# Blocks of edges two at a time on VectorE, one three-sum combine of x, and one addition for an odd tile's k and v

## The chip, the core and the metric

One core of one Trainium2 chip runs the whole kernel. The engines are named as in the profile: PE is TensorE's matmul, PEld its weight load, DVE is VectorE, ACT is ScalarE, POOL is GpSimd (it issues the indirect DMAs, the gathers and scatters by row number), SP is SyncE (it issues plain DMAs). The metric is the device time of one execution in microseconds; the median of several runs counts.

## The reference

Graph attention with a residual and a layer norm, for 16 batches of 1024 nodes with 512 features and 8 heads of 64. The adjacency is one matrix of zeros and ones for all batches. It is sparse and skewed: node i's chance of an edge falls with its number.

```python
q, k, v = (x @ W + b).reshape(b, n, H, HD)  for W, b of q, k and v
scores = einsum('bqhd,bkhd->bhqk', q, k) / sqrt(HD)
scores = scores + (1.0 - adj)[None, None, :, :] * -1000000000.0
attn = softmax(scores, axis=-1)
out = einsum('bhqk,bkhd->bqhd', attn, v).reshape(b, n, d)
x = layernorm(x + out @ Wo + bo, axis=-1)
```

## The kernel before

The kernel does not build the 1024 x 1024 scores. It sorts the nodes by their number of edges, at the start and on the chip, and then works on **blocks**: one block is 128 edges, one for each of 128 query nodes, so a block needs 128 rows of q on the 128 partitions and the 128 rows of k and v at the other ends of the edges, which POOL gathers from DRAM. There are 530 blocks over the 16 batches, in a list `blocks`. A block's steps, with the tiles they write:

- `gather(n)`: POOL fetches a `kvg` tile of 128 rows, k in columns 0 to 511 and v in the rest. It is issued eight turns ahead (`AHEAD`). The tag `kvg` has 8 buffers.
- `products(n)`: DVE multiplies q (`qt`, or `qg` where it was gathered as well) with k into `qk`, line 1313.
- `scores(n)`: DVE sums that by head, 128 x 512 to 128 x 8, into `s`, line 1317.
- `exponentials(n)`: ACT, into the last 8 columns of a `pv` tile, line 1328.
- `weigh(n)`: v times these, by ACT in 8 instructions (line 1341) or by DVE in one (line 1345).
- `add_own(n)` on DVE (line 1357) or `add_up(n)` as two matmuls on PE (`sum`, lines 1366 and 1367) put a tile's blocks together; `normalise` divides, a transpose makes `oT`, and four matmuls with `wo` (`po`, line 799) and the layer norm finish the tile.

**PE's other half** is q, k and v for all rows. q is four matmuls a tile (`pq`, also line 799). For k and v, two tiles of 128 rows (`pair(b, j)`, tiles 2j and 2j + 1 of batch b, four pairs a batch) go together in a scheme of seven half products in place of eight: combinations of the weights (`t1` to `t4`) and of x (`s1` to `s4`, each 128 x 256, made in `combine` by four DVE instructions, lines 783 to 786) are made beforehand, and afterwards DVE adds the results up. Each half product is two matmuls of 128 x 512, four records in the trace. They go in this order, with what follows each on another engine one turn later:

- x (`b11`), then ACT copies it to `e` (line 969)
- p6 (`t2`), then DVE makes `w` = p6 + e (line 972)
- the four matmuls of q of the even tile
- x (`b21`) on top of the first, then ACT copies the even tile's k out of it (line 835)
- p7 (`t3`), then DVE makes `g` = p7 + w (line 975)
- transposes of the next pair's x (`pxT`)
- z (`t1`), then the odd tile's v = z + g (line 984)
- the four matmuls of q of the odd tile (none in the first pair of a batch after the first)
- p4 (`t4`), then the odd tile's k = p4 + g (line 979)
- z (`b22`) on top of the first z, once line 984 has read it, then the even tile's v = z + w (line 988)

x and z are one PSUM tile each, with one buffer; p6, p7, p4 and everything else share four `fill` banks; `sum` has two.

**What sets the order.** The program is written out by a loop over turns n. In each turn the steps above are issued for blocks near n in a fixed order (exponentials of n + 3, products of n + 4, gathers, weighing of n + 1, adding of n, scores of n + 4, then whatever earlier steps planned for this turn with `later`), and then PE gets matmul units from two lists, `finishing` (`po`) and `fronts` (the pairs), as many as its share of the turn allows. A unit is issued only when its `ready` condition holds. The engines then run their lists strictly in order, and semaphores set by the tile framework hold them where a tile isn't written or free.

Of the kernel before, what the change touches and what calls it, by code (L numbers as in the profile page):

```python
# [31 lines left out]
KG_BUFS, Q_BUFS, QT_BUFS, PV_BUFS, Y_BUFS = 8, 5, 3, 5, 6  # L32
# [146 lines left out]
def kernel(  # L179
# [75 lines left out]
    with ExitStack() as main:  # L255
# [101 lines left out]
        def loads():  # L357
# [26 lines left out]
            nc.vector.tensor_tensor(T2, B22, T1, op=OP.subtract)  # L384
            combined.append(True)
            yield
            nc.vector.tensor_tensor(T3, B22, B12[0], op=OP.subtract)
# [73 lines left out]
        def ranks():  # L461
            yield
            for t in range(NT):
                ADJ.append(work.tile([P, N], F32, tag="kvg", name=f"adj_{t}", bufs=KG_BUFS))
                nc.gpsimd.dma_start(ADJ[t], adj[ds(t * P, P), :])
# [171 lines left out]
        def edges(t):  # L637
            nb, J, K = BLOCKS[t], DEGREE[t], OWN[t]
            tag, bufs = ("kvg", KG_BUFS) if J > 16 else ("kv", 5)
            v = work.tile([P, N], F32, tag=tag, name=f"codes_{t}", bufs=bufs)  # L640
# [60 lines left out]
            for i0 in range(0, nb, step):  # L701
# [8 lines left out]
                m = work.tile([P, D], F32, tag="qk", name=f"em_{t}_{i0}", bufs=2)[:, 0:n * J].rearrange("p (n j) -> p n j", n=n)  # L710
# [27 lines left out]
        X, XT, SX, KV, VSUM, NRM, Y, OT, PS = {}, {}, {}, {}, {}, {}, {}, {}, {}  # L738
# [13 lines left out]
        def transpose_x(b, t):  # L752
            def pe():
# [5 lines left out]
                def out():  # L759
                    XT[b, t] = work.tile([P, D], F32, tag="xT", name=f"xT_{b}_{t}", bufs=4)  # L760
# [19 lines left out]
                def combine():  # L780
                    s = [work.tile([P, HD2], F32, tag=f"s{i}", name=f"s{i}_{b}_{t}", bufs=1 + i // 4) for i in (1, 2, 3, 4)]
                    x0, x1 = XT[b, t - 1], XT[b, t]
                    nc.vector.tensor_tensor(s[0], x1[:, 0:HD2], x1[:, HD2:D], op=OP.add)
                    nc.vector.tensor_tensor(s[2], x0[:, 0:HD2], x1[:, 0:HD2], op=OP.subtract)
                    nc.vector.tensor_tensor(s[1], s[0], x0[:, 0:HD2], op=OP.subtract)
                    nc.vector.tensor_tensor(s[3], x0[:, HD2:D], s[1], op=OP.subtract)
                    SX[b, t // 2] = s
# [23 lines left out]
        def norm(b, t, k):  # L811
            if b not in NRM:
                NRM[b] = work.tile([P, NT, NPAIR], F32, tag="nrm", name=f"nrm_{b}", bufs=2)
            squares(f"k_{b}_{t}", k, NRM[b][:, t, :])

        def pair(b, j):
# [131 lines left out]
            def unit(bank, left, right, first, after, need):  # L948
                def pe():
                    if first:  # L950
                        R[bank] = fill_psum(f"p{bank}_{b}_{j}") if bank[0] == "p" else psum.tile(
                            [P, HALF], F32, tag=bank, name=f"{bank}_{b}_{j}", bufs=1
                        )
# [8 lines left out]
                return [(2 * PRODUCT, pe, lambda: (need is None or need in R) and (b, j) in SX and bool(combined))]  # L962
# [13 lines left out]

            def out_k1():
                kv = KV[b, tt[1]]
                nc.vector.tensor_tensor(kv[:, 0:D], R["p4"], R["g"], op=OP.add)  # L979
                send(1)  # L980
                later_last(1, lambda: norm(b, tt[1], kv[:, 0:D]))
# [5 lines left out]
            def out_v0():  # L987
                nc.vector.tensor_tensor(KV[b, tt[0]][:, D:], R["z"], R["w"], op=OP.add)
                send(0)
# [5 lines left out]
            units += unit("x", lambda: a(0, 0), B11, True, out_e, None)  # L995
            units += unit("p6", s(2), T2, True, out_w, None)
            units += q0
            units += unit("x", lambda: a(0, 1), B21, False, lambda: out_k(0, R["x"]), "e")
            units += unit("p7", s(3), T3, True, out_g, None)
            units += xt  # L1000
            units += unit("z", s(1), T1, True, out_v1, None)
            units += q1
            units += unit("p4", lambda: a(1, 1), T4, True, out_k1, None)
            units += unit("z", s(4), B22, False, out_v0, "v1")
            return units

        loaded, half, wide = {}, [], []
# [196 lines left out]
        KG, QG, PV, PSUM, QT, RDEN, V1 = {}, {}, {}, {}, {}, {}, {}  # L1204
# [45 lines left out]
        def gather(n):  # L1250
# [33 lines left out]
            else:  # L1284
                g = first[t] + i - OWN[t]
                tag, bufs = ("qt", Q_BUFS) if fronts or i % 2 else ("xT", 4)
                QG[n] = work.tile([P, D], F32, tag=tag, name=f"qg_{n}", bufs=bufs)
                gather_q(QG[n], b, (query_row if b else query_row0)[:, g:g + 1])
            tag, bufs = ("kvg", KG_BUFS) if fronts or n % 5 % 2 == 0 else ("kv", 5)
            KG[n] = work.tile([P, 2 * D], F32, tag=tag, name=f"kvg_{n}", bufs=bufs)  # L1290
# [9 lines left out]
        QK = {}  # L1300

        def products(n):
            b, t, i = blocks[n]
            if t == 0 and i == 0 and b < PAIRED_FROM:
                norms = small.tile([P, NPAIR], F32, tag="lone", name=f"lone_{b}", bufs=1)
                later_last(0, lambda q=QT[b, t]: squares(f"q_{b}", q, norms, lone))
                later(2, lambda: nc.vector.tensor_reduce(lone_norm[:, b:b + 1], norms, axis=AX.X, op=OP.max))
            if i < OWN[t]:
                q = QT[b, t] if i < OWN[t] - 1 else QT.pop((b, t))
            else:  # L1310
                q = QG.pop(n)
            QK[n] = work.tile([P, D], F32, tag="qk", name=f"qk_{n}", bufs=2)
            nc.vector.tensor_tensor(QK[n], q, KG[n][:, 0:D], op=OP.mult)  # L1313
# [344 lines left out]
```

## Time and profile before

| what | value |
|---|---|
| three timed runs | 1853.99, 1860.07, 1872.71 us, median 1860.07 |
| span of the profiled execution | 1840.4 us (its own time outside the span is not given) |
| busy PE, DVE, ACT, POOL | 1798.2, 1693.7, 1563.2, 1215.3 us |
| granted PE clock, mean | 0.996 |
| DMA | 303 GB/s, mean |

The span runs from the first to the last instruction of the profiled execution; the timed runs also hold what lies around it. Busy times are unions of the instructions' spans, and neighbouring instructions of one engine overlap at their ends, so the start-to-start distance, not the duration, tells what an instruction costs in a row.

### The profile page before, as it was taken

What the parts mean: (1) busy time and instruction counts of PE and PEld (TensorE: products, weight loads), DVE (VectorE), ACT (ScalarE), POOL (GpSimd) and SP (SyncE); (2) the same over time, 40 slices, a digit from 0 to 9 for tenths busy, and PEclk for the clock granted to TensorE, in tenths of its full rate; (3) what the DMA queues carried; (4) which work ended last, traced back from release to release, by engine and by line L of the source; (5) the groups of instructions that cost most, each with busy time, mean ns of one, the idle gap of its engine ahead of it and who ended that gap; (6) DMA issues with size and microseconds to landing.
All of it is one profiled execution on the core that took longest, in us unless ns stands there. A gap on an engine that the chain in (4) does not pass through costs nothing.

```text
span 1840.4 us, 25352 instructions
## 1 busy us (share of the span) xinstructions
PE 1798.2 (98%) x5140; PEld 876.2 (48%) x5140; DVE 1693.7 (92%) x3473; ACT 1563.2 (85%) x6183; POOL 1215.3 (66%) x1142
## 2 busy tenths in 40 slices
PE   7999999999999999999999999999999999999997
PEld 3444454554444454444444445444544444444443
DVE  6889889999989999999999999999999999997986
ACT  3637869989889898999889988989799999987886
POOL 1367766766565776767757666677666767665786
PEclk9999999999999999999999999999999999999998
DMA  7358787989889899999988998999989999889995
GB/s 287 106 190 253 256 325 237 346 301 327 308 280 314 295 336 319 344 316 308 347 316 310 346 335 276 343 321 322 339 315 325 314 355 326 306 324 325 338 319 191
DMA packets 198791, 558.54 MB, mean 303 GB/s; under 512 B 33450, under 2 KB 33470, under 8 KB 198626
## 3 DMA queue, kind: packets, MB, share of 16 engines
q0 software_dynamic: 112640, 370.50, 59.3%
q1 hardware_dynamic: 82910, 180.52, 26.2%
q10 hardware_dynamic: 3076, 5.82, 0.9%
q14 instruction: 122, 1.00, 0.2%
q8 instruction: 43, 0.70, 0.2%
HBM read 420.30 MB, written 157.45 MB: 314 GB/s over the span
## 4 chain that ended last, share of the span: by engine, by line
PE 69%; DVE 10%; ACT 9%; DMA 4%; issue 3%; POOL 1%; SPq 0%; POOLq 0%; DVEq 0%; ACTq 0%
PE po L799 17%; PE pq L799 15%; PE pp L956 12%; PE z L956 9%; PE x L956 9%; ACT pv L1341 5%; DVE qk L1313 2%; PE poT L1401 2%; PE pxT L757 2%; PE sum L1367 2%; DVE s L1317 2%; PE sum L1366 2%; DVE pv L1357 1%; ACT sq_k L809 1%; DMA kvg<-kv_pair,place_row 1%
## 5 line engine op out<-in xcount | busy, mean ns | idle before, releaser
L1341 ACT ACTIVATE pv<-kvg,pv 128x64 f32<-128x64 f32 x3600 | 907.5, 341 | 0.0
L1292 POOL DMA_INDIRECT kvg<-kv_pair,place_row x462 | 526.7, 1140 | 307.4 <-ACT pv L1341 99.6
L799 PE MATMUL pq<-wq,xT 128*128 128x512 f32 x792 | 367.8, 596 | 0.0
L1317 DVE TENSOR_REDUCE s<-qk 128x8 f32<-128x512 f32 x530 | 360.7, 681 | 6.8
L799 PE MATMUL po<-wo,oT 128*128 128x512 f32 x792 | 359.3, 594 | 0.7 <-ACT oT L1405 0.7
L1313 DVE TENSOR_TENSOR qk<-qt,kvg 128x512 f32<-128x512 f32 x434 | 297.2, 685 | 1.1 <-DMA kvg<-kv_rows,key_row 0.6
L956 PE MATMUL x<-b,xT 128*128 128x512 f32 x504 | 237.3, 593 | 0.5 <-ACT e L969 0.4
L956 PE MATMUL pp<-t,s 128*128 128x512 f32 x504 | 237.0, 593 | 0.0
L1357 DVE TENSOR_TENSOR pv<-pv,pv 128x520 f32<-128x520 f32 x329 | 228.3, 694 | 4.3 <-ACT pv L1341 4.2
L799 PEld LDWEIGHTS po<-wo,oT 128*128 128x128 f32 x792 | 149.1, 191 | 170.0 <-issue 160.2
L799 PEld LDWEIGHTS pq<-wq,xT 128*128 128x128 f32 x792 | 148.4, 192 | 161.9 <-issue 149.9
L1010 POOL DMA_INDIRECT x<-in_x_dram,asked_row x120 | 133.0, 1108 | 77.8 <-issue 21.3
L1148 POOL DMA_INDIRECT out_dram<-y,asked_row x129 | 146.9, 1139 | 39.1 <-issue 21.2
L1328 ACT ACTIVATE pv<-s,absent 128x8 f32<-128x8 f32 x434 | 127.0, 294 | 44.0 <-DVE s L1317 40.8
L809 ACT ACTIVATE sq_k<-kv 128x128 bf16<-128x128 f32 x512 | 150.8, 301 | 6.4 <-DVE kv L979 3.4
L956 PEld LDWEIGHTS pp<-t,s 128*128 128x128 f32 x504 | 94.7, 191 | 108.1 <-issue 99.4
L956 PEld LDWEIGHTS x<-b,xT 128*128 128x128 f32 x504 | 94.2, 191 | 107.4 <-issue 99.0
L956 PE MATMUL z<-b,s 128*128 128x512 f32 x252 | 119.2, 596 | 7.0 <-DVE kv L984 7.0
L1246 POOL DMA_INDIRECT qg<-q_rows,query_row x96 | 104.4, 1088 | 28.4 <-issue 26.9
L956 PE MATMUL z<-t,s 128*128 128x512 f32 x252 | 118.6, 593 | 0.0
L956 PE MATMUL pp<-t,xT 128*128 128x512 f32 x252 | 118.5, 593 | 0.0
L1134 ACT ACTIVATE y<-y,stats 128x512 f32<-128x512 f32 (+1 forms) x128 | 102.7, 806 | 17.0 <-DVE stats L1129 17.0
(279 smaller groups left out, 2713.0 us busy)
## 6 DMA issues: line engine op xcount, KB each, us to landing
kv_pair<-kv SPq DMA_DIRECT2D x98, 512.0 KB
q_rows<-q SPq DMA_DIRECT2D x106, 256.0 KB
qt<-q_rows SPq DMA_DIRECT2D x98, 256.0 KB
residual<-x SPq DMA_DIRECT2D x83, 256.0 KB
y<-residual SPq DMA_DIRECT2D x83, 256.0 KB
kv_rows<-kv SPq DMA_DIRECT2D x15, 512.0 KB
kvg<-kv_pair,place_row POOLq DMA_INDIRECT x462, 6.9
kv_pair<-kv SPq DMA_DIRECT2D x28, 256.0 KB
```

What stands on the lines that cost most here:

```text
L799: nc.tensor.matmul(p, lhs(c), w[:, c, :], start=(c == 0), stop=(c == NPAIR - 1))
L809: nc.scalar.activation(sq, s[:, ts(h, P)], AF.Square, scale=scale, accum_out=sums[:, h:h + 1])
L956: nc.tensor.matmul(R[bank], l[:, ts(c, P)], right[:, c, :], start=(first and c == 0), stop=(c == 1), skip_group_check=True,)
L1010: nc.gpsimd.indirect_dma_start(out=y, out_offset=None, in_=x_rows, in_offset=bass.IndirectOffsetOnAxis(ap=asked_row[:, t:t + 1], axis=0), ...
L1148: nc.gpsimd.indirect_dma_start(out=out_rows[b, t], out_offset=bass.IndirectOffsetOnAxis(ap=rows, axis=0), in_=y, in_offset=None, element_o ...
L1246: nc.gpsimd.indirect_dma_start(out=q, out_offset=None, in_=q_rows[b % ROWS], in_offset=bass.IndirectOffsetOnAxis(ap=rows, axis=0))
L1292: nc.gpsimd.indirect_dma_start(out=KG[n], out_offset=None, in_=rows, in_offset=bass.IndirectOffsetOnAxis(ap=(place_row if b else key_row)[ ...
L1313: nc.vector.tensor_tensor(QK[n], q, KG[n][:, 0:D], op=OP.mult)
L1317: nc.vector.tensor_reduce(S[n], QK.pop(n).rearrange("p (h d) -> p h d", d=HD), axis=AX.X, op=OP.add)
L1328: nc.scalar.activation(PV[n][:, D:], S.pop(n), AF.Exp, bias=bias)
L1341: nc.scalar.activation(pv[:, ts(h, HD)], v[:, ds(D + h * HD, HD)], AF.Copy, scale=pv[:, D + h:D + h + 1])
L1357: nc.vector.tensor_tensor(PV[b, t], PV[b, t], pv, op=OP.add)
```

## The change

Three things change, and with them the tiles that carry them.

**Blocks two at a time.** `kvg` tiles become pairs, 4 of twice the size. `products` is called at odd turns for the blocks n + 3 and n + 4. Where both have the same q, one DVE instruction multiplies 128 x 2 x 512; otherwise two do. The product is written over k in `kvg`, and `qk` goes. `scores` sums both blocks in one instruction (128 x 16). Exponentials come at n + 2, after which the weighing by ACT follows in the same turn; gathers move behind DVE's weighing.

**Three sums of x.** The signs are turned so that s1 and s3 have one operand in common and can be made by one instruction of 2 x 256 into a tile `s31`. The transposed x of both tiles, too, lies in one tile of two halves.

**One addition for k and v.** x and z become the two halves of one PSUM tile `xz`, made once for the whole kernel. In the last three pairs of a batch p4 goes into the x half instead of a fill bank, moves ahead of z (`t1`), and one DVE instruction adds g to both halves, 1024 columns, into the odd tile's k and v. The first pair keeps two additions. A list `freed` tells `ready` that the step that reads a half has been issued.

The diff, cut to the parts that the prediction speaks of:

```diff
+        XZ = psum.tile([P, 2, HALF], F32, tag="xz", name="xz", bufs=1)
+        freed = []
...
-                    s = [work.tile([P, HD2], F32, tag=f"s{i}", name=f"s{i}_{b}_{t}", bufs=1 + i // 4) for i in (1, 2, 3, 4)]
-                    x0, x1 = XT[b, t - 1], XT[b, t]
-                    nc.vector.tensor_tensor(s[0], x1[:, 0:HD2], x1[:, HD2:D], op=OP.add)
-                    nc.vector.tensor_tensor(s[2], x0[:, 0:HD2], x1[:, 0:HD2], op=OP.subtract)
-                    nc.vector.tensor_tensor(s[1], s[0], x0[:, 0:HD2], op=OP.subtract)
-                    nc.vector.tensor_tensor(s[3], x0[:, HD2:D], s[1], op=OP.subtract)
+                    nc.vector.tensor_tensor(
+                        s31, both[:, :, 0:HD2], both[:, 1, :].rearrange("p (a d) -> p a d", a=2), op=OP.subtract
+                    )
+                    nc.vector.tensor_tensor(s2, both[:, 0, 0:HD2], s31[:, 1, :], op=OP.subtract)
+                    nc.vector.tensor_tensor(s4, both[:, 0, HD2:], s2, op=OP.subtract)
...
-                    if first:
-                        R[bank] = fill_psum(f"p{bank}_{b}_{j}") if bank[0] == "p" else psum.tile(
-                            [P, HALF], F32, tag=bank, name=f"{bank}_{b}_{j}", bufs=1
-                        )
+                    if first and bank in at:
+                        R[bank] = XZ[:, at[bank], :]
+                    elif first:
+                        R[bank] = fill_psum(f"p{bank}_{b}_{j}")
...
-                return [(2 * PRODUCT, pe, lambda: (need is None or need in R) and (b, j) in SX and bool(combined))]
+                return [(2 * PRODUCT, pe, lambda: all(k in R or k in freed for k in need) and (b, j) in SX and bool(combined))]
+
+            at = {"x": 0, "z": 1, "p4": 0} if j else {"x": 0, "z": 1}
...
+            def out_kv1():
+                kv = new_kv(1)
+                nc.vector.tensor_tensor(
+                    kv.rearrange("p (w d) -> p w d", w=2), XZ, R["g"][:, None, :].to_broadcast([P, 2, D]), op=OP.add
+                )
...
             def out_v0():
                 nc.vector.tensor_tensor(KV[b, tt[0]][:, D:], R["z"], R["w"], op=OP.add)
+                freed.append(("v", b, j))
                 send(0)
...
-            units += xt
-            units += unit("z", s(1), T1, True, out_v1, None)
-            units += q1
-            units += unit("p4", lambda: a(1, 1), T4, True, out_k1, None)
-            units += unit("z", s(4), B22, False, out_v0, "v1")
+            if j:
+                units += q1[:1] + xt
+                units += unit("p4", lambda: a(1, 1), T4, True, lambda: None, ["k0"])
+                units += unit("z", s(1), T1, True, out_kv1, last_v)
+                units += q1[1:]
+            else:
+                units += xt
+                units += unit("z", s(1), T1, True, out_v1, last_v)
+                units += unit("p4", lambda: a(1, 1), T4, True, out_k1, [])
+            units += unit("z", s(4), B22, False, out_v0, ["v1"])
...
+            if len(pair) == 2 and n in PAIR and q[n] is q[n + 1]:
+                k = PAIR[n][:, :, 0:D]
+                nc.vector.tensor_tensor(k, q[n][:, None, :].to_broadcast([P, 2, D]), k, op=OP.mult)
...
-                if 0 <= n + 3 < total:
-                    exponentials(n + 3)
-                if 0 <= n + 4 < total:
-                    products(n + 4)
+                if 0 <= n + 2 < total:
+                    exponentials(n + 2)
+                if 0 <= n + 3 < total and n % 2:
+                    products(n + 3)
```

What the order of the instructions becomes, at three places.

PE, from the last products of one pair (batch 7, pair 0) to the first of the next, with the engines whose semaphores each row waits for; before:

```order
L956 MATMUL pp4_7_0_8286<-t4_105,xT_7_1_7948 128x512 [waits DVE_49]
L956 MATMUL pp4_7_0_8286<-t4_105,xT_7_1_7948 128x512
L956 MATMUL z_7_0_8283<-b22_101,s4_7_1_7984 128x512 [waits DVE_49]
L956 MATMUL z_7_0_8283<-b22_101,s4_7_1_7984 128x512
L956 MATMUL x_7_1_8360<-b11_99,xT_7_2_8256 128x512 [waits Activation_49]
L956 MATMUL x_7_1_8360<-b11_99,xT_7_2_8256 128x512
L1401 MATMUL poT_5_5_8363<-ident_58,o_5_5_8301 128x128 x4
```

and now:

```order
L969 MATMUL pp4_7_0_7567<-t4_105,xT_7_0_7249 128x512 [waits DVE_49]
L969 MATMUL pp4_7_0_7567<-t4_105,xT_7_0_7249 128x512
L969 MATMUL xz_257<-b22_101,s4_7_1_7318 128x512 [waits DVE_49]
L969 MATMUL xz_257<-b22_101,s4_7_1_7318 128x512
L969 MATMUL xz_257<-b11_99,xT_7_2_7538 128x512 [waits DVE_49,Activation_49]
L969 MATMUL xz_257<-b11_99,xT_7_2_7538 128x512
L1465 MATMUL poT_5_5_7634<-ident_58,o_5_5_7578 128x128 x4
```

The rows are the same products in the same order. The first product of the next pair (`b11`) waits for DVE as well: the count that it waits for is the one that the addition of the even tile's v, `kv_7_0<-xz,w`, reaches. Of the 62 pairs with one before them 33 have this wait. In the other 29 the product stands ahead of that addition in the program, and the addition waits for the product.

PE again, within the next pair (batch 7, pair 1), without the waits; before:

```order
L757 MATMUL pxT_7_5_8488<-ident_58,x_7_5_8332 128x128 x4
L956 MATMUL z_7_1_8493<-t1_102,s1_7_3_8334 128x512 x2
L799 MATMUL pq_7_3_8533<-wq_63,xT_7_3_8304 128x512
L1401 MATMUL poT_5_1_8535<-ident_58,v1_5_8006 128x128 x4
L799 MATMUL pq_7_3_8533<-wq_63,xT_7_3_8304 128x512 x3
L956 MATMUL pp4_7_1_8573<-t4_105,xT_7_3_8304 128x512 x2
L799 MATMUL po_5_2_8608<-wo_64,oT_5_2_7831 128x512 x4
L956 MATMUL z_7_1_8493<-b22_101,s4_7_3_8337 128x512 x2
```

and now:

```order
L763 MATMUL pxT_7_5_7749<-ident_58,x_7_5_7606 128x128 x4
L969 MATMUL xz_257<-t4_105,xT_7_2_7538 128x512 x2
L969 MATMUL xz_257<-t1_102,s31_7_3_7608 128x512 x2
L1465 MATMUL poT_5_1_7788<-ident_58,v1_5_7304 128x128 x4
L810 MATMUL pq_7_3_7742<-wq_63,xT_7_2_7538 128x512 x3
L810 MATMUL po_5_2_7861<-wo_64,oT_5_2_7153 128x512 x4
L969 MATMUL xz_257<-b22_101,s4_7_3_7610 128x512 x2
```

The `t4` product has moved ahead of the `t1` product, and one of q's four matmuls ahead of the transposes. Between the two products into z stand three matmuls of q and what `finishing` put there, where four and the `t4` product stood too.

DVE, at the first of these places, from the odd tile's additions to the even tile's v; before:

```order
L984 TENSOR_TENSOR kv_7_1_8307<-z_7_0_8283,g_7_0_8228 128x512
L979 TENSOR_TENSOR kv_7_1_8307<-pp4_7_0_8286,g_7_0_8228 128x512
L1313 TENSOR_TENSOR qk_191_8322<-qt_5_7_8010,kvg_191_8186 128x512
L1357 TENSOR_TENSOR pv_186_8182<-pv_186_8182,pv_187_8211 128x520
L1317 TENSOR_REDUCE s_191_8329<-qk_191_8322 128x8
L1123 TENSOR_SCALAR stats_8223<-stats_8223 128x1
L783 TENSOR_TENSOR s1_7_3_8334<-xT_7_3_8304 128x256
L784 TENSOR_TENSOR s3_7_3_8336<-xT_7_2_8256,xT_7_3_8304 128x256
L785 TENSOR_TENSOR s2_7_3_8335<-s1_7_3_8334,xT_7_2_8256 128x256
L786 TENSOR_TENSOR s4_7_3_8337<-xT_7_2_8256,s2_7_3_8335 128x256
L988 TENSOR_TENSOR kv_7_0_8226<-z_7_0_8283,w_7_0_8091 128x512
```

and now:

```order
L1017 TENSOR_TENSOR kv_7_1_7583<-xz_257,g_7_0_7511 128x512
L1003 TENSOR_TENSOR kv_7_1_7583<-pp4_7_0_7567,g_7_0_7511 128x512
L1364 TENSOR_TENSOR kvg_190_7438<-qt_5_7_7308,kvg_190_7438 128x2x512
L1421 TENSOR_TENSOR pv_186_7498<-pv_186_7498,pv_187_7528 128x520
L1374 TENSOR_REDUCE s_190_7603<-kvg_190_7438 128x16
L1162 TENSOR_SCALAR stats_7506<-stats_7506 128x1
L792 TENSOR_TENSOR s31_7_3_7608<-xT_7_2_7538 128x512
L795 TENSOR_TENSOR s2_7_3_7609<-xT_7_2_7538,s31_7_3_7608 128x256
L796 TENSOR_TENSOR s4_7_3_7610<-xT_7_2_7538,s2_7_3_7609 128x256
L1021 TENSOR_TENSOR kv_7_0_7509<-xz_257,w_7_0_7384 128x512
```

This is an odd turn: the product and the sum of block 191 have become those of 190 and 191. In the turn before it, block 190's have gone. The three sums of x stand where the four stood, each needing the one before it.

In all DVE has 3176 instructions instead of 3695. PE's matmuls are the same but for one small one, and ACT, POOL and SP issue what they issued.

116 lines of the change are left out of this document (80 added, 36 removed).

## The prediction

> **What bounds the kernel now.** I read the head of the page first, then the busy time by stretch, and then the instructions one by one.
>
> ```profile
> span 1840.4 us, 25352 instructions
> PE 1798.2 (98%) x5140; PEld 876.2 (48%) x5140; DVE 1693.7 (92%) x3473; ACT 1563.2 (85%) x6183; POOL 1215.3 (66%) x1142
> ```
>
> PE is busy for 98% of the span, DVE for 92%. Both look full, so the stretch between the start and the tail has to say which of the two sets the time.
>
> ```profile
> core 0: us, PE busy (x) PEld busy (x) DVE busy (x) ACT busy (x) POOL busy (x), PEclk, DMA share, GB/s
> 184.00:1748.00 1564.00, 1549.71 (x4461) 759.07 (x4460) 1477.34 (x2931) 1394.06 (x5641) 1061.44 (x977) 1.00 0.91 317
> ```
>
> In these 1564 us PE is idle for 14.3 us at the full granted clock, and DVE for 87. So PE sets the pace, and it is a row of matmuls in a fixed order. A change to DVE can win at most these 14.3 us and something at the two ends. It can lose much more: whatever PE must newly wait for is added to the span one for one. The question is therefore what PE waits for. One place shows how the two engines stand to each other, first PE, then DVE (columns: start, duration, engine, line, operation, tiles, count, idle before):
>
> ```profile
> 757.49 1.88 PE L956 MATMUL pp<-t,xT 128*128 128x512 f32 x4
> 759.53 1.98 PE L956 MATMUL z<-b,s 128*128 128x512 f32 x4 [0.16 <-DVE kv L984]
> 761.35 1.88 PE L956 MATMUL x<-b,xT 128*128 128x512 f32 x4
> 763.07 0.60 PE L1401 MATMUL poT<-ident,o 128*128 128x128 f32 x4
> ```
> ```profile
> 758.79 0.68 DVE L984 TENSOR_TENSOR kv<-z,g 128x512 f32<-128x512 f32 x1
> 759.41 0.69 DVE L979 TENSOR_TENSOR kv<-pp,g 128x512 f32<-128x512 f32 x1
> 763.42 0.68 DVE L988 TENSOR_TENSOR kv<-z,w 128x512 f32<-128x512 f32 x1
> ```
>
> Four records of one product (two matmuls) take 1.72 us from start to start. The second product into z waits for L984, which ends at 759.47; PE starts at 759.53, so a release costs 0.06 us. Then the first product of the next pair (x) follows at once, at 761.35, although L988 does not read z before 763.42. DVE is 2.0 us late here and nobody minds, because x and z are two tiles.
>
> ```profile
> L956 PE MATMUL z<-b,s 128*128 128x512 f32 x252 | 119.2, 596 | 7.0 <-DVE kv L984 7.0
> L984 DVE TENSOR_TENSOR kv<-z,g 128x512 f32<-128x512 f32 x63 | 43.2, 686 | 13.9 <-PE z L956 13.1
> L988 DVE TENSOR_TENSOR kv<-z,w 128x512 f32<-128x512 f32 x63 | 42.9, 681 | 1.4 <-PE z L956 1.4
> ```
>
> The groups say the same of all 63 pairs: PE waited 7.0 us in all for L984. L988 was hardly ever ready early: DVE idled 1.4 us before it in the whole run. Over the 62 pairs with a successor it starts 0.04 to 6.45 us after z's last matmul ends, with a median of 1.9.
>
> **The change part by part.** *Merged instructions on DVE.* The trace has a run of independent additions of each width:
>
> ```profile
> 42.44 1.21 DVE L387 TENSOR_TENSOR t<-b,b 128x1024 f32<-128x1024 f32 x1
> 43.57 1.22 DVE L388 TENSOR_TENSOR t<-b,t 128x1024 f32<-128x1024 f32 x1
> ...
> 703.95 0.41 DVE L783 TENSOR_TENSOR s<-xT 128x256 f32<-128x256 f32 x1
> 704.28 0.42 DVE L784 TENSOR_TENSOR s<-xT,xT 128x256 f32<-128x256 f32 x1
> 704.62 0.42 DVE L785 TENSOR_TENSOR s<-s,xT 128x256 f32<-128x256 f32 x1
> 705.07 0.42 DVE L786 TENSOR_TENSOR s<-xT,s 128x256 f32<-128x256 f32 x1
> 705.41 0.68 DVE L830 SCALAR_TENSOR_TENSOR q<-pq,bq_bc 128x512 f32<-128x512 f32 x1
> 706.01 0.68 DVE L1313 TENSOR_TENSOR qk<-qt,kvg 128x512 f32<-128x512 f32 x1
> ```
>
> Durations overlap, so I go by starts: 1.13 us for 1024 elements, 0.60 for 512, 0.335 for 256, and 0.45 where an instruction needs the one just before it (L785 to L786). A merge of two 512 into one 1024 saves 2 x 0.60 - 1.13 = 0.07 us. The new program has 259 doubled reductions, 150 doubled products and 48 doubled additions for k and v: 457 x 0.07 = 32 us. The trace has no doubled reduction and none that reads both products; they lie between 1.13 and 1.20 us, so the saving between 0 and 32, and I take 1.13, the nearest row. The four sums of x take 1.46 us (703.95 to 705.41). Three take 0.60 + 2 x 0.45 = 1.50, since each now needs the one before it. They win nothing. DVE thus gets about 30 us of its 1694 back, some 0.5 us per pair of tiles, beside a PE that does not wait for most of it.
>
> *The second product into z (term b).* The order shows that for three pairs in four, PE now has three matmuls of q (2.57 us) between the two z products, where it had four and the T4 product (5.15 us) or more. The new addition of k and v also ends some 0.5 us later than L984 did. With DVE's delays of before, pair by pair, PE would wait 19 us in place of 7. With each addition 0.5 us earlier, by the 30 us above, it is 13. I take +6 us; the ends are -7 (no wait left) and +24 (each addition 0.6 us later).
>
> *The first product of the next pair (term a).* This is the part that matters. x and z become the halves of one tile xz that lives through the whole kernel. In the order the first product into the x half carries a wait on DVE that it did not have, and the count it waits for is reached by L988's successor, the addition that reads the z half of the pair before. That is so in 33 of the 62 places. In the other 29 the product stands ahead of the addition in the program, and then the addition waits for the product, at most 1.72 us of DVE, which has room. In the 33, 21 have no PE work between the second z product and x, 5 have a group of transposes or one block's sum (0.44 or 0.87 us), and 7 have 3.4 to 4.3 us. The first and the last of the 33, PE then DVE:
>
> ```profile
> 116.02 1.98 PE L956 MATMUL z<-b,s 128*128 128x512 f32 x4
> 117.84 1.88 PE L956 MATMUL x<-b,xT 128*128 128x512 f32 x4
> ...
> 1648.04 1.88 PE L956 MATMUL z<-b,s 128*128 128x512 f32 x4
> 1649.75 3.60 PE L799 MATMUL po<-wo,oT 128*128 128x512 f32 x8
> 1653.19 1.88 PE L956 MATMUL x<-b,xT 128*128 128x512 f32 x4
> ```
> ```profile
> 119.46 0.68 DVE L988 TENSOR_TENSOR kv<-z,w 128x512 f32<-128x512 f32 x1
> ...
> 1650.06 0.68 DVE L988 TENSOR_TENSOR kv<-z,w 128x512 f32<-128x512 f32 x1
> ```
>
> In the first, L988 ends at 120.14, PE could go on at 120.20 instead of 117.84: 2.36 us lost. In the last, eight records of po lie between and hide it. At 757 us above it is 763.42 + 0.68 + 0.06 - 761.35 = 2.81. Done for all 33 this gives 66 us, 57 of them from the 21 that stand bare. The lower end is that DVE already stands waiting at each: 0.04 to start, 0.68, 0.06, and 0.16 by which a matmul's end lies behind the next one's start, so 0.95 a time: 21 x 0.95, and almost nothing for the rest, is 20 us. The upper end is the lag with the doubled instructions in front of the addition. In turns that hold a pair's product and reduction, DVE has 1.06 us more before it, in the others as much less; at the worst half a microsecond more on each, 79 us. I take 53: the lag as traced, less 0.5 us at each. That is nearer to the traced rows than to the floor, since DVE was early at L988 in 3 places of 63 only. Behind a stopped PE stands everything else on its queue, so nothing hides it.
>
> *Other edits.* The fourth product (T4) takes the x bank for a fill bank; it waits for ACT's copy of k, with at least 3.4 us of PE work between. Exponentials stand one turn later, gathers behind the weighing, and products are written in place: these move work between DVE, ACT and POOL, which all have idle time in the row above, and feed PE through sums that come turns later. I count them at nothing; without that cover they would show as PE waits on pv. DVE's 0.5 us per pair also shortens the other waits of PE: 14.3 less 7.0 is 7.3 us, and I give 6 of it back.
>
> *The sum.* 53 + 6 - 6 = +53 us on the profiled span: 1840.4 becomes about 1893. The page gives no time of its own beside its span; the three timed runs lie 13.6 to 32.3 us above it, the median, 1860.07, 19.7. The change goes onto the median: 1913 us.
>
> **The rivals.** *DVE is early (same).* If PE's stops let DVE catch up for good, each wait at x falls to its floor, 20 us in all, the waits at z fall to 5 (-2), and the 6 us of relief stay: 20 - 2 - 6 = +12, so 1872 us. It decides at a mean lag of some 0.3 us: 21 x (0.91 + 0.3) = 25, less 8 is 17 us, just inside 1%. For it: every stop gives DVE time. Against it: L988's place in its turn stands behind products, weighing and reductions that need nothing of PE. Chance 0.17.
>
> *The lighter DVE pays (not slower).* If the wait on the other half cost nothing at all, because its count were reached earlier than I read it, the rest is 6 - 6 = 0, and at best all 14.3 us of idle PE go: 1846 to 1860 us. No lag decides this one, since the addition ends 0.95 us too late even with DVE ready, only whether the wait is there. Chance 0.05, and only luck at the tail would make it over 1%. [...]
>
> *The clock halves as well (slower still).* Near the end of the trace PE stands idle for 3 us, and the clock follows:
>
> ```profile
> 1808.33 1.02 PE L1401 MATMUL poT<-ident,o 128*128 128x128 f32 x4 [3.09 <-DVE stats L1123]
> 1809.14 3.25 PE L799 MATMUL po<-wo,oTs 128*128 128x512 f32 x4
> ```
> ```profile
> 1809.00:1815.00 6.00, 6.00 (x15) 3.02 (x14) 4.80 (x14) 4.70 (x14) 4.03 (x5) 0.76 0.40 142
> ```
>
> Four matmul records took 3.25 us instead of 1.88, and the granted clock of that stretch (the last number but two) is 0.76, so such an idle time costs 1.4 us more. Of the 33 waits 8 are over 3 us at the traced lag. If each halves the clock, that is 11 us: 1924 with my lag, 1950 with the longer one. Chance 0.13. [...]
>
> **How the numbers follow.** Forecast (1885 to 1940) 0.63, DVE early (1860 to 1880) 0.17, lighter DVE 0.05, clock or longer lags (1940 to 1965) 0.15. The range takes the upper half of the second case and the lower half of the last: 1872 to 1946. One per cent, about what a measurement of this kernel tells from no change, is 18.6 us. Slower by more than that: the forecast, the last case and a little of the second, 0.78. Within it 0.18, faster 0.04.
>
> **What would show it.** PE waits on DVE at the x half of xz, some 25 times and 1 to 3.5 us each, 40 to 65 us in all; PE's matmul counts as before; busy PE in the middle stretch down from 99% to about 96; DVE's busy time some 60 us or less lower, since overlapping ends vanish with merged instructions; the combine group no shorter; waits at the second z product 5 to 15 us. I am wrong if PE's waits at x are below 20 us, or if PE shows new waits on pv or on gathers, which I put at nothing.

## The result, and the profile after

The changed kernel takes 2015.67 us (median; 2011.5 to 2018.26), the kernel before 1859.19 in the same comparison: a ratio of **1.0836**, 95% interval 1.0789 to 1.0883. The forecast was 1913, with a range of 1872 to 1946. The direction and the first mechanism were right, the size was not: +156 us where +53 was forecast. The profiled execution took 2017.64 us, 1.8 more than its span of 2015.8; the span of before was 1840.4, so there are 175 us of span to account for.

The head of the page, and the groups of PE, DVE and ACT that the prediction spoke of (busy time, mean of one, idle time before them and what ended it):

```profile
span 2015.8 us, 24697 instructions
PE 1851.0 (92%) x5139; PEld 884.5 (44%) x5139; DVE 1665.3 (83%) x2954; ACT 1588.3 (79%) x6183; POOL 1233.4 (61%) x1143
L969 PE MATMUL xz<-b,xT 128*128 128x512 f32 x504 | 260.4, 642 | 66.3 <-DVE kv L1021 31.3
L969 PE MATMUL xz<-b,s 128*128 128x512 f32 x252 | 129.4, 638 | 41.5 <-DVE kv L1009 33.3
L1374 DVE TENSOR_REDUCE s<-kvg 128x16 f32<-128x1024 f32 x259 | 314.1, 1213 | 2.6
L988 ACT COPY e<-xz 128x512 f32<-128x512 f32 x63 | 36.7, 582 | 176.8 <-DVE kv L1021 105.3
```

The group of the third line in the kernel before:

```profile
L956 PE MATMUL x<-b,xT 128*128 128x512 f32 x504 | 237.3, 593 | 0.5 <-ACT e L969 0.4
```

Every engine is less busy by share: all of them wait. PE's two new waits stand in the third and fourth line: 66.3 us before products into the x half (`b11` and `b21`), against 0.5, and 41.5 us before the second product into z, against 7.0. DVE is 28 us less busy, and idle 17% of the span. The steady part shows the second loss, the clock (PE's busy time first, the granted clock is the last number but two):

```profile
184.00:1920.00 1736.00, 1614.00 (x4508) 774.88 (x4507) 1466.98 (x2485) 1433.87 (x5707) 1091.23 (x988) 0.98 0.85 288
```

PE is busy for 93% where it was 99%, and the granted clock is 0.98 where it was 1.00. One place shows how the two losses hang together: the end of a pair and the start of the next, first PE, then DVE.

```profile
834.18 1.98 PE L969 MATMUL xz<-b,s 128*128 128x512 f32 x4
840.58 3.75 PE L969 MATMUL xz<-b,xT 128*128 128x512 f32 x4 [4.42 <-ACT pv L1405]
844.13 1.06 PE L1465 MATMUL poT<-ident,o 128*128 128x128 f32 x4
```
```profile
835.29 1.23 DVE L1364 TENSOR_TENSOR kvg<-qt,kvg 128x1024 f32<-128x1024 f32 x1 [0.36 <-DMA kvg<-kv_pair,place_row]
836.44 0.69 DVE L1421 TENSOR_TENSOR pv<-pv,pv 128x520 f32<-128x520 f32 x1
837.05 1.21 DVE L1374 TENSOR_REDUCE s<-kvg 128x16 f32<-128x1024 f32 x1
838.18 0.14 DVE L1162 TENSOR_SCALAR stats<-stats 128x1 f32<-128x1 f32 x1
838.24 0.68 DVE L792 TENSOR_TENSOR s<-xT 128x512 f32<-128x512 f32 x1
838.95 0.43 DVE L795 TENSOR_TENSOR s<-xT,s 128x256 f32<-128x256 f32 x1
839.41 0.42 DVE L796 TENSOR_TENSOR s<-xT,s 128x256 f32<-128x256 f32 x1
839.75 0.68 DVE L1021 TENSOR_TENSOR kv<-xz,w 128x512 f32<-128x512 f32 x1
```
```profile
839.50:846.33 6.83, 5.75 (x10) 2.91 (x11) 2.14 (x4) 4.09 (x19) 4.67 (x5) 0.50 0.99 348
```

The second z product is over at 836.16. L1021, which reads it, stands behind the seven instructions listed above it, six of which start after that, and ends at 840.43; PE starts the next pair's first product at 840.58. The profile names ACT's weighing (its last instruction ends at 840.53) as what ended this wait, but the product does not read what the weighing writes. DVE's addition is what it waits for: in 27 of the 33 places PE starts 0.06 or 0.15 us after that addition's end; in the other six the addition had been over for longer. From 839.5, about a microsecond before the stop ends, the clock is granted at 0.50 for 6.83 us, and four records take 3.75 us instead of 1.88.

To compare kernels I took from each trace, for every matmul record, how much later than its shape's full-speed spacing it starts (0.43 us for 128x512, 0.11 for a transpose), and summed the places above 0.15 us. What records lose by the slower pace inside stretches of half clock is counted apart, in the last column. "Other stops" holds `b21` too. "Ratio" is to runs of the kernel before on the same chip, with its 95% interval. That kernel took 1845 to 1875 us on the chips used, so the last two columns compare only roughly between chips.

| kernel | ratio | stops at x (`b11`) | at the second z product | other stops | half clock |
|---|---|---|---|---|---|
| before | 1 | 0.3 us | 7.8 | 26 | 3.1 |
| after | 1.0836 [1.0789, 1.0883] | 68.1 (31 places) | 46.2 (26) | 52 | 38.2 |
| `e8_one_tile`: one tile xz alone | 1.0405 [1.0336, 1.0475] | 58.1 | 7.2 | 35 | 21.8 |
| `e3_two_tiles`: all but the one tile | 1.0335 [1.0268, 1.0403] | 0.9 | 42.7 | 57 | 17.2 |
| `e2_only_kv`: third part alone | 1.0756 [1.0683, 1.0829] | 58.2 | 57.7 | 42 | 31.3 |
| `e1_no_kv`: first two parts | 1.0086 [1.0052, 1.0120] | 0.5 | 5.9 | 54 | 7.9 |
| `e5_blocks`: blocks alone | 1.0111 [1.0095, 1.0126] | 0.8 | 7.2 | 48 | 10.3 |
| `e6_sums`: sums alone | 1.0017 [1.0006, 1.0029] | 0.3 | 8.5 | 29 | 5.5 |
| `e16_x_first`: one tile, v written later | 1.0061 [1.0039, 1.0083] | 0.6 | 7.5 | 60 | 10.5 |
| `e18_x_first`: the same in the change | 1.0405 [1.0371, 1.0439] | 0 | 56.1 | 64 | 20.8 |

Of the 175 us, 68 are new stops at x, 38 new stops at z, 26 other stops, and 35 half clock; 8 are not accounted for.

### The profile page after: what moved, and what is told of

Read it like the earlier page. It is cut to its first block, busy times and chain, and to the rows that moved or that the text cites. A ratio compares the mean times of both kernels' runs of the same rounds, so it can differ in the third digit from the quotient of the medians.

```text
span 2015.8 us, 24697 instructions
## 1 busy us (share of the span) xinstructions
PE 1851.0 (92%) x5139; PEld 884.5 (44%) x5139; DVE 1665.3 (83%) x2954; ACT 1588.3 (79%) x6183; POOL 1233.4 (61%) x1143
## 5 line engine op out<-in xcount | busy, mean ns | idle before, releaser
L1340 POOL DMA_INDIRECT kvg<-kv_pair,place_row x462 | 539.3, 1167 | 472.9 <-ACT pv L1392 155.2
L810 PE MATMUL pq<-wq,xT 128*128 128x512 f32 x792 | 374.7, 596 | 0.9 <-DVE s L1374 0.9
L969 PE MATMUL xz<-b,xT 128*128 128x512 f32 x504 | 260.4, 642 | 66.3 <-DVE kv L1021 31.3
L1374 DVE TENSOR_REDUCE s<-kvg 128x16 f32<-128x1024 f32 x259 | 314.1, 1213 | 2.6
L969 PE MATMUL pp<-t,s 128*128 128x512 f32 x504 | 242.0, 603 | 2.6 <-DVE t L384 1.5
L1364 DVE TENSOR_TENSOR kvg<-qt,kvg 128x1024 f32<-128x1024 f32 x150 | 182.6, 1217 | 6.8 <-DMA kvg<-kv_pair,place_row 6.7
L969 PEld LDWEIGHTS xz<-b,xT 128*128 128x128 f32 x504 | 98.2, 203 | 194.8 <-issue 126.5
L988 ACT COPY e<-xz 128x512 f32<-128x512 f32 x63 | 36.7, 582 | 176.8 <-DVE kv L1021 105.3
L969 PE MATMUL xz<-b,s 128*128 128x512 f32 x252 | 129.4, 638 | 41.5 <-DVE kv L1009 33.3
L969 PE MATMUL xz<-t,s 128*128 128x512 f32 x252 | 119.7, 597 | 0.0
```

The lines of the kernel that those rows point to most:

```text
L810: nc.tensor.matmul(p, lhs(c), w[:, c, :], start=(c == 0), stop=(c == NPAIR - 1))
L969: nc.tensor.matmul(R[bank], l[:, ts(c, P)], right[:, c, :], start=(first and c == 0), stop=(c == 1), skip_group_check=True,)
L1340: nc.gpsimd.indirect_dma_start(out=KG[n], out_offset=None, in_=rows, in_offset=bass.IndirectOffsetOnAxis(ap=(place_row if b else key_row)[ ...
L1364: nc.vector.tensor_tensor(k, q[n][:, None, :].to_broadcast([P, 2, D]), k, op=OP.mult)
L1374: nc.vector.tensor_reduce(s, k.rearrange("p w (h d) -> p w h d", d=HD), axis=AX.X, op=OP.add)
```

## The experiments

**Which part costs it.** Theory 1 was that waits on the whole of xz are the loss, theory 2 that the new order of the units is, theory 3 that the blocks are. Four kernels, of which `e1_no_kv` undoes the third part, `e2_only_kv` does it alone, `e3_two_tiles` keeps the new order but parts the tile, and `e8_one_tile` joins the tile but keeps the order of before.

```diff
 e1_no_kv, to the changed kernel
-                        R[bank] = XZ[:, at[bank], :]
+                        R[bank] = fill_psum(f"p{bank}_{b}_{j}") if bank[0] == "p" else psum.tile(
+                            [P, HALF], F32, tag=bank, name=f"{bank}_{b}_{j}", bufs=1
+                        )
...
 e2_only_kv, to the kernel before
+        XZ = psum.tile([P, 2, HALF], F32, tag="xz", name="xz", bufs=1)
...
+                    if first and bank in at:
+                        R[bank] = XZ[:, at[bank], :]
...
 e3_two_tiles, to the changed kernel
-                        R[bank] = XZ[:, at[bank], :]
+                        R[bank] = psum.tile([P, HALF], F32, tag="xz"[at[bank]], name=f"{bank}_{b}_{j}", bufs=1)
...
-                nc.vector.tensor_tensor(
-                    kv.rearrange("p (w d) -> p w d", w=2), XZ, R["g"][:, None, :].to_broadcast([P, 2, D]), op=OP.add
-                )
+                nc.vector.tensor_tensor(kv[:, D:], R["z"], R["g"], op=OP.add)
+                nc.vector.tensor_tensor(kv[:, 0:D], R["p4"], R["g"], op=OP.add)
...
 e8_one_tile, to the kernel before
+        XZ = psum.tile([P, 2, HALF], F32, tag="xz", name="xz", bufs=1)
...
-                        R[bank] = fill_psum(f"p{bank}_{b}_{j}") if bank[0] == "p" else psum.tile(
-                            [P, HALF], F32, tag=bank, name=f"{bank}_{b}_{j}", bufs=1
-                        )
+                        R[bank] = fill_psum(f"p{bank}_{b}_{j}") if bank[0] == "p" else XZ[:, "xz".index(bank), :]
```

> The changed kernel with its third part undone: x and z are two PSUM tiles again, p4 is in a fill bank, the units stand in the old order and the odd tile's k and v come by two additions. Blocks two at a time and the three sums of x stay. Theory 1 (the waits on the whole of xz are the loss) and theory 2 (the new order of the units is): no loss left, 1845 to 1865 us. Theory 3 (blocks two at a time make exponentials, gathers and weighing late): 1960 us or more, with PE's stops at x and z still there.

> The kernel before with the third part alone: xz as one tile for the whole kernel, p4 in its x half and ahead of t1, one addition for the odd tile's k and v. Single blocks and four sums as before. Theories 1 and 2: the whole loss, 1990 to 2040 us. Theory 3: little of it, 1850 to 1890.

> The changed kernel with x and z as two PSUM tiles (p4 in a new x tile), so that no reader of the one is held by the other, and with two additions where the one needed both in one tile. The order of the units is the new one, with three matmuls of q between the products into z. Theory 1: the stops at x go, and most of those at the second z product too, 1855 to 1885 us. Theory 2: the stops at the second z product stay at 40 us or more, 1910 us or more.

> The kernel before with one edit: x and z are the halves of one PSUM tile that lives through the whole kernel. Order, additions, blocks and sums are those of before. The first product of a pair then waits for the even tile's v addition in 31 places, and ACT's copy e in 55. Theory 1: most of the loss by this alone, 1940 to 2020 us (some 70 us of stops at x, the rest at z and by the clock). Theory 2: the forecast's term alone, at most +53 us, 1915 us or less. Theory 3: no loss.

Measured: 1.0086, 1.0756, 1.0335 and 1.0405. `e1_no_kv`, at 1882 us, is 17 us above its range: the first two parts cost something. The groups of the products into x and of the second product into z, of `e8_one_tile` and then of `e3_two_tiles`:

```profile
L955 PE MATMUL xz<-b,xT 128*128 128x512 f32 x504 | 252.6, 625 | 56.1 <-DVE kv L987 30.6 <-issue 12.2 <-DVE s L1316 4.6
L955 PE MATMUL xz<-b,s 128*128 128x512 f32 x252 | 120.3, 600 | 6.2 <-DVE kv L983 3.2 <-DVE s L787 3.0
```
```profile
L968 PE MATMUL x<-b,xT 128*128 128x512 f32 x504 | 241.3, 602 | 1.6 <-ACT e L987 1.6
L968 PE MATMUL z<-b,s 128*128 128x512 f32 x252 | 127.9, 632 | 38.3 <-DVE kv L1008 30.0 <-issue 4.2 <-DVE kv L1015 3.2
```

Each of the two carries one stop and not the other: one tile makes the stops at x, the new order those at z. Theories 1 and 2 are both half right, and neither alone reaches the loss: 4.05% and 3.35% (0.9% of which is the first two parts) stand against 8.36%. Where either theory had the other's stop follow from its own, it was wrong. Joining the tiles is enough for the wait; the doubled addition that reads both halves has no visible share in it (58.1 us of stops at x in `e8_one_tile` without it, 58.2 in `e2_only_kv` with it). Theory 3 holds for 0.9%.

**The first two parts one by one.**

```diff
 e5_blocks, to the kernel before
-                if 0 <= n + 4 < total:
-                    products(n + 4)
+                if 0 <= n + 3 < total and n % 2:
+                    products(n + 3)
...
 e6_sums, to the kernel before
-                    nc.vector.tensor_tensor(s[0], x1[:, 0:HD2], x1[:, HD2:D], op=OP.add)
...
+                        s31, both[:, :, 0:HD2], both[:, 1, :].rearrange("p (a d) -> p a d", a=2), op=OP.subtract
```

> The kernel before with the first part alone: blocks two at a time, gathers behind DVE's weighing, exponentials one turn later. Four sums and the old k and v. The run with the second part undone too was 0.9% over the kernel before. If the blocks cost that: 1.005 to 1.012 of the kernel before, with PE's new stops spread over pxT, pq, pm and po. If the sums do: 0.997 to 1.003.

> The kernel before with the second part alone: three sums of x instead of four, the transposed x of a pair of tiles in one tile. The forecast has this at nothing (1.46 us become 1.50): 0.997 to 1.003. If the longer chain from the last xT to s4 delays PE: 1.005 or more, with stops at p6 and at the second z product.

Measured: 1.0111 [1.0095, 1.0126] and 1.0017 [1.0006, 1.0029]. The sums cost nothing that matters. The blocks cost 1%, with PE's stops spread, as expected. A likely reason was in DVE's rows: before its products DVE waited 1.9 us in all for gathers in the kernel before; with pairs it is more (all three groups):

```profile
L1324 DVE TENSOR_TENSOR kvg<-qt,kvg 128x1024 f32<-128x1024 f32 x150 | 182.8, 1219 | 8.9 <-DMA kvg<-kv_pair,place_row 5.5 <-DMA kvg<-kv_rows,key_row 1.9 <-issue 1.4
L1327 DVE TENSOR_TENSOR kvg<-qt,kvg 128x512 f32<-128x512 f32 x134 | 89.9, 684 | 7.2 <-DMA kvg<-kv_pair,place_row 4.3 <-DMA kvg<-kv_rows,place_row 2.9
L1327 DVE TENSOR_TENSOR kvg<-qg,kvg 128x512 f32<-128x512 f32 x96 | 65.8, 687 | 10.4 <-DMA kvg<-kv_pair,place_row 9.2 <-DMA kvg<-kv_rows,place_row 1.1
```

Two more kernels tested it, with buffers of `qt` and `pv` given up for a fifth pair of `kvg`:

```diff
 e12_five_pairs, to e5_blocks (e13_four_pairs: 4, 4, 3, 4, 6 and AHEAD = 8)
-AHEAD = 8
-KG_PAIRS, Q_BUFS, QT_BUFS, PV_BUFS, Y_BUFS = 4, 5, 3, 5, 6
+AHEAD = 9
+KG_PAIRS, Q_BUFS, QT_BUFS, PV_BUFS, Y_BUFS = 5, 4, 3, 4, 6
```

> The kernel with blocks two at a time alone (1.011 of the kernel before, DVE idle 26 us before its products for gathers) with five pair buffers and gathers nine turns ahead instead of four and eight; to make room qt and pv have four buffers instead of five. If late buffers make the gathers late and these the loss: DVE's wait before products falls to 8 us or less and the time to 1.000 to 1.005. If not: 1.009 or more.

> The same with four pair buffers and eight turns, so that only the fewer buffers of qt and pv differ from the kernel with blocks two at a time alone: 1.010 to 1.016 if these cost little, more if they cost something by themselves.

Measured: 1.0131 [1.0084, 1.0178] and 1.0076 [1.0048, 1.0104], the second below its range. With five pairs the wait for gathers went entirely (two of the three groups; the third has 0.0 as well):

```profile
L1324 DVE TENSOR_TENSOR kvg<-qt,kvg 128x1024 f32<-128x1024 f32 x150 | 182.6, 1217 | 0.0
L1327 DVE TENSOR_TENSOR kvg<-qg,kvg 128x512 f32<-128x512 f32 x96 | 65.6, 685 | 0.0
```

The time did not: five pairs are no faster than four. Late gathers were not the loss of the blocks. What it is stays open; that every second turn now holds all of a pair's work on DVE, and PE's fill banks come free later in it, is only argued.

**The stops at z: cover or place.** In the new order PE has less between the two z products, a median of 3.0 us against 5.6. The odd tile's v addition also ends later, 2.3 us after the first z product in `e3_two_tiles` (median) and 1.6 in the kernel before. Cover is the PE work between the two products, lag the time until the addition ends. Pair by pair the lags of before with the new covers would give about 13 us of stops, the new lags with the old covers about 4, and both together about 40, by a sum worked out from the traces of the two kernels. Two kernels took one each.

```diff
 e10_cover4, to e3_two_tiles
-                units += q1[:1] + xt
+                units += xt
...
-                units += q1[1:]
+                units += q1
 e7_head, to the changed kernel (e14_order_head, to e3_two_tiles: out_kv1 alone)
-                    later(1, after)
+                    (later_first if after in (out_v0, out_kv1) and "g" in R else later)(1, after)
...
+                for fn in head.pop(n, ()):
+                    fn()
```

> The changed kernel with DVE's two additions out of xz (the doubled one, and the even tile's v) moved from their place in the turn to the head of it, before exponentials' successors, products and weighing. Waits and order of PE stay. If DVE's place in its turn makes the stops: at x they fall to about their floor of 20 to 25 us, at the second z product to 15 or less, and with them the half-speed clock; 1890 to 1925 us. If DVE is merely short of time, so that the stops come back at pq, pm, poT and sum: 1970 us or more.

> The kernel with x and z as two tiles in the new order (1930 us), with one edit: the four matmuls of q of the odd tile stay together between the two products into z, where the first of them stood ahead of the transposes. The cover of the second z product grows from 2.57 to 3.43 us at least. If the short cover is the whole of the order's loss: stops at the second z product fall from 43 us to 20 to 28, 1900 to 1915 us, and p4, which now comes 0.86 us sooner, waits no longer than 5 us for ACT's copy of k. If something else of the order costs it: 1925 us or more.

> The changed kernel with x and z as two tiles in the new order (1.0335 of the kernel before, 43 us of stops at the second z product), and the odd tile's two additions at the head of their turn. If DVE's place in its turn makes these stops: 12 us or less of them, 1.010 to 1.022 of the kernel before. If the new order costs through something else: 1.028 or more.

Measured: `e10_cover4` 1.0303 [1.0287, 1.0319], with 36.9 us of stops at z where 20 to 28 were expected: the addition came later still (2.5 us, median), so more cover alone does not do it. (Its time, 1901 us, is in the range given, but on a chip where the kernel before takes 1845 us; the ratio hardly fell from 1.0335.) `e7_head` 1.0604 [1.0585, 1.0623]: stops at x fell from 68 to 32 us (20 to 25 were expected) and at z from 46 to 15, as expected, but other stops rose to 78 (52 in the changed kernel, 39 in `e10_cover4` on the same chip), and the time, 1957 us, is above the 1890 to 1925 given for the place in the turn. `e14_order_head` 1.0435 [1.0401, 1.0469] is slower than without the edit (1.0335), where 1.010 to 1.022 was given. In both, the additions stand ahead of everything else in the turn. The rows of `e14_order_head`, three of PE and one of DVE, show where the time went. Behind them stand the last three without the edit, of `e3_two_tiles`; its line of z is shown above, with 38.3 us.

```profile
L971 PE MATMUL z<-b,s 128*128 128x512 f32 x252 | 127.6, 631 | 22.6 <-DVE kv L1011 13.9 <-DVE kv L1018 5.9 <-issue 2.9
L1466 PE MATMUL poT<-ident,o 128*128 128x128 f32 x420 | 65.0, 278 | 32.5 <-DVE o L1452 11.6 <-DVE stats L1169 10.3 <-DVE rden L1448 8.6
L765 PE MATMUL pxT<-ident,x 128*128 128x128 f32 x512 | 73.1, 278 | 25.7 <-DVE q L845 9.0 <-DMA x<-in_x_dram 6.7 <-DVE g L996 2.5
L1011 DVE TENSOR_TENSOR kv<-z,g 128x512 f32<-128x512 f32 x48 | 33.1, 690 | 92.0 <-PE z L971 53.1 <-issue 24.4 <-remote 14.1
```
```profile
L1463 PE MATMUL poT<-ident,o 128*128 128x128 f32 x420 | 63.8, 275 | 11.4 <-DVE stats L1160 8.0 <-ACT pv L1403 1.9 <-DVE stats L1166 1.5
L762 PE MATMUL pxT<-ident,x 128*128 128x128 f32 x512 | 71.6, 277 | 13.7 <-DMA x<-in_x_dram 6.7 <-DVE q L842 3.5 <-DVE y L1149 1.6
L1008 DVE TENSOR_TENSOR kv<-z,g 128x512 f32<-128x512 f32 x48 | 32.9, 686 | 20.5 <-PE z L968 15.8 <-remote 3.7 <-issue 1.0
```

At the head of the turn DVE stands still for 92 us in front of this addition, where it did for 20.5, and what is queued behind it is late: `poT` and `pxT` wait for DVE's `o` and `q`. The place in the turn does size the stops, but moving it trades one stop for another: DVE's idle time was no slack. Why the addition starts later in the new order at all (1.64 us after the first z product's end, median, for 0.86) is not shown.

**The stops at x: place, or who waits for whom.** Both kernels take `e8_one_tile`.

```diff
 e15_tile_head, to e8_one_tile
-                    later(1, after)
+                    (later_first if after is out_v0 else later)(1, after)
 e16_x_first, to e8_one_tile (e18_x_first: to the changed kernel)
-                    later(1, after)
+                    if after is out_v0 and (b, j) != (B - 1, NT // 2 - 1):
+                        pending.append(after)
+                    else:
+                        later(1, after)
+                    if first and bank == "x" and pending:
+                        later(1, pending.pop())
```

> The kernel before with x and z as one tile (1.0405 of the kernel before, 58 us of stops at x), and the even tile's v addition at the head of its turn instead of behind products, weighing and reductions. If DVE's place in its turn sizes the stops at x: 20 to 30 us of them are left, by the floor of 0.95 us at each of 21 bare places, and the clock's loss falls with them; 1.010 to 1.022 of the kernel before. If DVE is short of time whatever the place: 1.033 or more.

> The kernel before with x and z as one tile, and the even tile's v addition written behind the next pair's first product and ACT's copy e in all 62 places, as the forecast had it harmless in 29 of them. The addition then waits for ACT's copy, and the next product into x (b21) for the addition, with q's four matmuls and p6 (5.15 us) between. If the forecast's step holds that DVE can wait there at no cost: stops at x below 8 us, 0.998 to 1.010. If a waiting DVE makes the others late: 1.02 or more, with stops at pq, pm, poT and at the second product into x.

> The changed kernel with one edit: the even tile's v addition is written behind the next pair's first product and ACT's copy e in all 62 places. Stops at x (68 us) fall to 5 or less. If the tile's loss and the order's add up: what the new order costs with two tiles, 1.030 to 1.042 of the kernel before. If the stops move to another place: 1.055 or more.

Measured: `e15_tile_head` 1.0249 [1.0219, 1.0280]: stops at x 29.5 us, as expected, but the time is above the range. `e16_x_first` 1.0061 [1.0039, 1.0083], in its range, on the same chip; against it `e15_tile_head` has 29 us more of stops at x, 12 more of others (72) and 5 more of half clock, 46 for the 46.7 us between the two profiled spans (the medians lie 39 us apart). The place has its price in other stops again. All products into the x half in `e16_x_first`, `b21` too, which now carries the wait:

```profile
L956 PE MATMUL xz<-b,xT 128*128 128x512 f32 x504 | 241.3, 602 | 7.1 <-DVE kv L993 5.6 <-issue 1.4
```

So the shared tile need not cost much; its 4% was which of the two had to wait. In the changed kernel the same edit takes all 68 us at x away and the ratio from 1.0836 to 1.0405 [1.0371, 1.0439], the upper end of what adding up had given; the stops at z stay (56 us).

**Both mends.** The edit of `e16_x_first` and that of `e14_order_head` in the changed kernel:

> The changed kernel with both edits: the even tile's v addition behind the next pair's first product, the odd tile's doubled addition at the head of its turn. Everything that the change does is still in it, the same matmuls and the doubled instructions. If the two kinds of stops and the clock that follows them are the loss beside that of the blocks (1.0086 to 1.011): 1.010 to 1.022 of the kernel before, and no more than 20 us of stops at x and z. If DVE is short of time: 1.035 or more.

Measured: 1.0491 [1.0438, 1.0543], a miss. Stops at z fell to 31 us, and other stops rose to 95 (64 in `e18_x_first`, on the same chip, without the second edit). The rival that was written down gave 1.035 or more: with the doubled addition waiting at the head of its turn, DVE is short of time. No kernel of these was faster than the kernel before.

## Why the prediction was wrong, step by step

PE's losses grew by 167 us where the sum had 53. Of the 114 us between, 15 are in term (a), 32 in term (b), 32 in the other edits and the relief (26 us of new stops where 6 us were given back), and 35 in the clock, which the sum left out. The step that failed is the sizing: the waits were priced with DVE's lags of the kernel before, less a relief, and what the change itself makes later, and the half clock behind the stops, was put at nothing.

- **PE is the bound, and a wait on PE costs one for one**: held. The sum of PE's losses, 68 + 38 + 26 + 35 = 167 us, gives the 175 us of span but for 8.
- **Term (a), the first product of the next pair**: the mechanism and its places held (33 forecast, 31 stops seen). Its size was 68 us for 53. The lag as traced gave 66; the half microsecond that I took off each, since DVE was to be lighter, was wrong. The even tile's v started 2.2 us after the end of the z product (median) instead of 1.9.
- **Term (b), the second product into z**: mis-sized, 38 us for 6, the larger error of the two terms. The step that failed is "With DVE's delays of before, pair by pair": the addition ended 2.85 us after the end of the first z product (median) where it had ended after 1.55. The sum had 0.5 us of that, for the doubled addition, and took it off again as relief; the rest is a later start, 1.64 us for 0.86. `e3_two_tiles` shows it without the shared tile, `e2_only_kv` without the merged blocks.
- **The 29 places where the addition waits for the product, at no cost**: held. `e16_x_first` makes it 62 places for 0.6%. What I did not see is that ACT's copy e, too, waits for the addition; the page has 105.3 us of ACT idle for it. PE's stops at `b21`, which comes after it, rose only from 0.5 to about 4 us.
- **Merges**: the prices held. Doubled instructions take 1.13 to 1.15 us from start to start (837.05 to 838.18, 835.29 to 836.44), the three sums 1.51 us (838.24 to 839.75). DVE's busy time fell by 28 us for "some 60 or less", and none of it came back: the relief of 6 us was wrong in sign, since other stops rose.
- **Other edits count at nothing**: wrong by some 16 to 20 us (`e1_no_kv` 0.9%, `e5_blocks` 1.1%). The cover I named, that all three engines have idle time, was no cover. No long waits on pv, by which I would have known it, appeared; the added stops are mostly at pxT and poT in the changed kernel, and at pxT, pq, pm and po in `e1_no_kv`.
- **The clock rival** was no rival but part of the outcome: 35 us, priced at 11. I let only waits over 3 us at x count; shorter ones did it too (9 of 18 stops between 2 and 3 us), and there were 57 stops at x and z, not 33. **DVE early** and **the lighter DVE pays** did not come true: PE's stops at x came to 68 us, where the one had 20 and the other none. The range's ends, 1872 and 1946, are not quite the halves that it names (1870 and 1952.5); that changes nothing here.

## To carry to other kernels

Where the bounding engine gains a wait, price it at the lag that the trace shows, and expect lags to grow where the order changes, as from 1.55 to 2.85 us here; ask first whether the program can be written so that the other engine is the one that waits, as moving one addition behind the next product turned 4.05% into 0.6%. Idle time of a feeding engine need not be slack: in `e14_order_head` an instruction that waited at the head of its turn, 92 us in all where it was 20.5, delayed what stood behind it. And joining two tiles to save an instruction joined their waits: those of PE at one half, and those of ACT's copy, on DVE's reading of the other (58 us of stops at x in `e8_one_tile`, and 105 us of ACT idle before `e` in the changed kernel).

## What the runs showed of the hardware

In the changed kernel the granted clock fell to 0.50 after shorter stops than the 3.09 us seen before. From 184 to 1990 us half speed began between the start of a stop and 2 us after its end for 11 of 12 stops of 3 us and more, 9 of 18 between 2 and 3 us, and at most 1 of 20 between 1 and 2 us. This one was 2.29 us, in the row of PE, then the windows of the stop and of what came after it:

```profile
571.88 2.50 PE L969 MATMUL xz<-b,s 128*128 128x512 f32 x4 [2.29 <-DVE kv L1009]
```
```profile
569.00:573.00 4.00, 1.71 (x5) 0.64 (x4) 3.97 (x8) 0.00 (x0) 3.39 (x3) 1.00 0.47 151
573.20:576.61 3.41, 3.41 (x5) 1.35 (x4) 1.68 (x2) 0.00 (x0) 1.69 (x3) 0.50 0.88 267
```

All 20 half-speed stretches that begin there last 3.41 us or a multiple of it: 13 last 3.41 us, six 6.83 and one 10.24. The length of a stop alone does not tell whether one follows: this stop of 2.29 us has one behind it, and the stop of 3.31 us that ended at 380.17 has none (a granted clock of 1.00 until 385.4). What else decides it was not shown.
